# Lists in layer 0 without waits among them, two tail masks on VectorE, and later expert tiles normalised by VectorE and ScalarE

## The chip, the core and the metric

The kernel runs on one core of a Trainium2 chip. The core has five instruction queues that run side by side and meet at semaphores: TensorE (PE, matrix products and transposes into PSUM), VectorE (DVE), ScalarE (ACT), GpSimd (POOL) and SyncE (SP, which here only starts transfers). Each executes its own instructions strictly in order. The metric is the device time of one launch in microseconds, the median of three runs.

## What is computed

The reference is a network of two "metaformer" layers on four images `x` (4, 256, 32, 32) in float32. With 256 channels there are 1024 tokens an image, 4096 in all.

```python
# layer 0
x = x + attention(ln_c(x))     # 8 heads; per row only the dyn_k largest scores stay, then softmax
                               # plus a 3x3 depthwise convolution of v, and a 1x1 projection
t = to_tokens(x)
t = t + moe0(ln_t(t))          # 8 experts 256->256->256 with gelu, each token to its best two
x = from_tokens(t)
# layer 1
x = x + scans(ln_c(x))         # selective scan in four directions, averaged
t = to_tokens(x)
t = t + moe1(ln_t(t))          # 8 experts with a layer norm each, 256->1024->256, best two
```

In the attention, `dyn_k` comes from the data: `dyn_k = floor(1024 * mean(sigmoid(gate(x))))`. `moe0` normalises the tokens before the router and the experts and adds its own input back: `out = tokens + sum of combine * expert(tokens)`.

## The kernel before

The program goes through four stages: attention with routing (0 to about 1975 us), the expert tiles of layer 0 (to about 2222), the scans of layer 1 (to about 3480), and the expert tiles of layer 1 (to the end). The change touches the first two.

**Attention.** The unit is a half: 128 query rows of an image by four heads, 64 halves in all. The order of work is written out by hand as turns `i = 0..71`. In turn `i`, half `i` gets its scores on TensorE, which ScalarE copies to SBUF (`s_n`). VectorE and ScalarE count how many scores lie above a guessed threshold, in this and the following turns (lines 733 and 737, each one pass over 128x1024 scores), and `update` narrows the guess. Half `i - 3` is then finished: VectorE runs `w` and `MAX8` over each of its four score rows (lines 784 and 787), and picks the exact threshold from the window (lines 792 to 798, the result is `last`). GpSimd makes four masks `dr` (line 817), one for each head, 128x1024 in bfloat16: one where the score lies below `last`. Six small operations on GpSimd, `verify` (lines 806 to 811), check the choice. In the next turns two halves of a group form a `Pair`. Its `weights` are computed on TensorE: products of q and k (line 872), onto which the masks are transposed and added as large negative numbers (line 877, with `dr` as the stationary operand). ScalarE takes the exponential (line 885), TensorE the sums (line 895), VectorE divides (lines 904 and 905). The masks of the odd half of a pair have one buffer each, those of the even half two. The last pair, 31, of halves 62 and 63, is made in turn 66.

**Lists.** Once an image is finished, its tokens are routed beside the attention of the following image; images 0, 1 and 2 start at turns 24, 40 and 56. When the places of its tokens are known, `send` (lines 210 to 217) writes the token rows to the slots of their experts, `slots_x0`: for each of 8 blocks of 128 tokens two indirect DMAs (first and second expert), issued by GpSimd. In `behind_masks`, which stands after masks and checks in a turn, images 0 and 1 send one block a turn over 8 turns, and image 2 two blocks a turn in turns 63 to 66. They are called with `group = None`: each such DMA then depends on the one before it, since both write `slots_x0`. The last image is routed after the attention, and its DMAs form a group without dependencies among them ("scatter0").

**Expert tiles of layer 0.** Tokens lie sorted by expert in tiles of 256; there are 36 of them (three more stand ready for very uneven routing and aren't run). Here an automatic scheduler orders the instructions from the program order and its estimates. A tile consists of: `load` (SP starts DMAs for the rows `xs` and the expert's weights, lines 1428 to 1433; `xs` has 6 buffers), `normed` (line 1438, GpSimd, two operations of 128x256 that scale and shift each row into `xn`, which has 2 buffers), `small` (weights of the two experts and biases, VectorE, lines 1449 to 1463), `turned` (four TensorE transposes, line 1445, and a VectorE copy to `xe`, line 1447), `hidden` (TensorE, line 1470, and gelu on ScalarE, line 1472), `result` (TensorE, line 1478; VectorE, line 1481) and `store` (ScalarE, line 1485: an Identity with a scale and a shift for each row; VectorE, line 1487; a GpSimd DMA to `rows_y0`, line 1489).

Other work stands beside the tiles (the loop at line 1948): from tile 14 on, the completion of image 0 and the preparation of its scans; from tile 22 on, that of image 1. To complete an image, `fetched` gathers its tokens' results with 16 indirect DMAs on GpSimd (line 1878), and `completed` transposes them on TensorE (`op`, line 1891) into `x` (VectorE, line 1897). The preparation of the scans (lines 1774 to 1843) uses all engines; it takes exponentials and logarithms on ScalarE between the tiles' gelus, which switches ScalarE's function tables (ACT_TABLE_LOAD).

Of the kernel before, what the change touches and what calls it, by code (L numbers as in the profile page):

```python
# [16 lines left out]
AF = mybir.ActivationFunctionType  # L17
ALU = mybir.AluOpType
# [4 lines left out]
B = 4  # L23
C = 256
# [3 lines left out]
NT = L // P  # L28
# [19 lines left out]
FIRST, SECOND = (2 * (i + 1) * L // T + E - 1 for i in range(2))  # L48
# [14 lines left out]
def metaformer(ctx: ExitStack, tc: tile.TileContext, t: dict, out: bass.AP):  # L63
    nc = tc.nc
# [145 lines left out]
    def send(b, tiles, group):  # L210

        for n in tiles:
            for k in range(2):
                ins = nc.gpsimd.indirect_dma_start(
                    out=slots_x0, out_offset=bass.IndirectOffsetOnAxis(ap=sent[:, k, b * NT + n : b * NT + n + 1],
                                                                       axis=0),
                    in_=xr[b][:, n], in_offset=None).ins
                if group is not None:
                    tc.declare_no_dep(ins, group=group, reason="rows of their own")
                    tc.add_to_no_dep_group(group, ins)  # L220

    def counted(sums, both, tiles):

# [246 lines left out]
    with ExitStack() as st:  # L470
# [23 lines left out]
        for j in range(4):  # L494
            r = slice(32 * j, 32 * j + 32)
# [224 lines left out]
        class Half:  # L720
# [76 lines left out]
                self.last = p2.tile([P, 4], F32, tag="last", name="last")  # L797
                nc.vector.tensor_reduce(self.last, pv, AX.X, ALU.add)

            def verify(self):  # L800


                win = self.win
                sure = p2.tile([P, 4, WIN + 2], F32, tag="sure", name="sure", bufs=1)
                pool = nc.gpsimd.tensor_tensor
                pool(sure[:, :, : WIN + 1], win[:, :, : WIN + 1], win[:, :, 1:], ALU.subtract)
                pool(sure[:, :, WIN + 1], win[:, :, 0], win[:, :, 2], ALU.subtract)
                nc.gpsimd.tensor_scalar(sure, sure, 0.0, None, ALU.is_gt)
                pool(sure[:, :, : WIN + 1], sure[:, :, : WIN + 1], self.hot, ALU.mult)
                pool(sure[:, :, WIN + 1], sure[:, :, WIN + 1], self.group.small[:, self.m], ALU.mult)  # L810
                pool(fine, fine, sure, ALU.add)

            def mask(self, after):
                self.drops = []
                for r in range(4):
                    dr = wk.tile([P, L], BF16, tag=f"dr{self.n}{r}", name="dr", bufs=2 - self.n)
                    ins = nc.gpsimd.tensor_scalar(dr, self.row(r), self.last[:, r : r + 1], None, ALU.is_lt)  # L817
                    if r == 0 and after is not None:

                        tc.add_manual_dep(ins.ins, after.ins.name,  # L820
                                          mybir.DependencyInfo(mybir.DependencyClass.Sync,
                                                               mybir.DependencyReason.DATA))
                    self.drops.append(dr)
# [84 lines left out]
        order = [(b, g, a, n) for b in range(B) for g in range(2) for a in range(NP) for n in range(2)]  # L908
# [13 lines left out]
        for b in range(B):  # L922
            i = b * PER
# [9 lines left out]
        routings = {}  # L933
# [4 lines left out]
        for b in range(B - 1):  # L938
            turn0 = b * PER + 24
# [4 lines left out]
        def behind_masks(i):  # L944
            for turn0, routing in routings.items():
                at = i - turn0
                if at == 1:
                    routing.spread((0, 1))
                if at == 2:
                    routing.spread((2, 3))  # L950
                    routing.root()
                if at == 4:
                    routing.shares()
                    routing.locate()
                if at == 6:
                    routing.fix()
                if routing.b < B - 2 and 7 <= at < 15:
                    send(routing.b, (at - 7,), None)
                if routing.b == B - 2 and 7 <= at < 11:
                    send(routing.b, (2 * at - 14, 2 * at - 13), None)  # L960

        def before_masks(i):
            for turn0, routing in routings.items():
# [53 lines left out]
        def turn(i):  # L1017
            def half(d):
                return halves[i - d] if 0 <= i - d < len(halves) else None

            h0, h1, h2, h3 = (half(d) for d in range(4))

            pair, q = pairs.get((i - 5) // 2 if i % 2 else (i - 6) // 2), 0 if i % 2 else 2
            done = pairs.get((i - 7) // 2) if i % 2 else None

            if h0:
                h0.scores(1)
                h0.take(0)
            before_masks(i)
            beside(i, 0)  # L1030
            if h0:
                h0.count(4, h0.at_guess, (0, 1))
                h0.take(1)
            if pair:
                pair.weights(q)
            if h3:
                h3.window(0)
                h3.window(1)
            if half(1) or half(2):
                to_u(slice(0, 2), FIRST_DVE[1])  # L1040
                update(stay=True)
            if h2:
                h2.keep_threshold()
            if done:
                done.norm()
            if h0:
                h0.count(4, h0.at_guess, (2, 3))
            beside(i, 1)
            if pair:
                pair.exps()  # L1050
                pair.sums(q)
            if h3:
                h3.window(2)
                h3.window(3)
                h3.select()
            if h1:
                h1.count(FIRST_DVE[0], h1.at_state)
            beside(i, 2)
            if pair:
                pair.weights(q + 1)  # L1060
            if h0:
                h0.enter()
            if h1:
                to_u(slice(h1.lane, h1.lane + 1), FIRST_DVE[0])
            after = update(stay=False) if h0 or h1 else None
            if h2:
                h2.count(FIRST_DVE[0], h2.at_last, (0, 1))
            if h3:
                h3.mask(after)
                h3.verify()  # L1070
                if h3.n == 1:
                    pairs[h3.i // 2] = Pair(halves[h3.i - 1 : h3.i + 1], images[h3.b])
            behind_masks(i)
            beside(i, 3)
            if pair:
                pair.exps()
            if h2:
                h2.count(FIRST_DVE[0], h2.at_last, (2, 3))
            if i + 1 < len(order):
                start(i + 1)  # L1080
            if pair:
                pair.sums(q + 1)
            beside(i, 4)
            if h0:
                h0.count(FIRST_DVE[1], h0.at_state)
            if h1:
                h1.count(FIRST_DVE[1], h1.at_state)
# [136 lines left out]
            due(1 << 20)  # L1224

        for h in range(NHALF):
            send(B - 1, range(4 * h, 4 * h + 4), "scatter0")

    def attention_by_bits(st):
        wp = st.enter_context(tc.tile_pool(name="a_w", bufs=1))  # L1230
# [170 lines left out]
    def tiles_of_0(st, name):  # L1401
# [13 lines left out]
        class Tile0:  # L1415
# [19 lines left out]
            def normed(self):  # L1435
                self.xn = pb.tile([P, T // P, C], F32, tag="xn", name="xn")
                for a in range(T // P):
                    nc.gpsimd.tensor_scalar(self.xn[:, a], self.xs[:, a, :C], self.xs[:, a, C + 4 : C + 5],
                                            self.xs[:, a, C + 3 : C + 4], ALU.mult, ALU.add)

            def turned(self):
                tp = ps1.tile([P, CT, T], F32, tag="tp", name="tp")
# [52 lines left out]
    with tc.If(some > 0):  # L1495
# [4 lines left out]
        with tc.If(again > 0):  # L1500
            with ExitStack() as st:
                attention_by_bits(st)
            with tc.tile_pool(name="g_w", bufs=1) as pool_s, tc.tile_pool(name="g_ps", bufs=4, space=PSUM) as pool_p:
                nc.sync.dma_start(slots_x0.rearrange("(a p) c -> p a c", p=P),
                                  blank(pool_s)[:, :W0].unsqueeze(1).to_broadcast([P, (E * BLOCKS + 1) * T // P, W0]))
                space = pool_s.tile([P, L], F32, tag="space", name="space")
                for b in range(B):
                    for h in range(NHALF):
                        wide_bank = pool_p.tile([P, L], F32, tag="w", name="wide_bank", bufs=2)
                        for _ in halved(b, h, space, lambda name: pool_p.tile([P, HALF], F32, tag="m", name=name),  # L1510
                                        lambda: wide_bank):
                            pass
                        send(b, range(4 * h, 4 * h + 4), "scatter0_again")
                for _ in table(space, lambda name: pool_p.tile([P, HALF], F32, tag="m", name=name)):
                    pass
        more_tiles = nc.values_load(extra[0:1, 0:1], min_val=0, max_val=1,
                                    skip_runtime_bounds_check_because="a comparison gives 0 or 1")
        with tc.If(more_tiles > 0):
            with ExitStack() as st:
                Tile0, _, _ = tiles_of_0(st, "mx")  # L1520
# [454 lines left out]
    with ExitStack() as st:  # L1975
# [100 lines left out]
        order = [(b, c, s) for b in range(B) for c in range(CT) for s in range(NS)]  # L2076
# [94 lines left out]
    with ExitStack() as st:  # L2171
# [71 lines left out]
        with ExitStack() as sa:  # L2243
# [16 lines left out]
            b = B - 1  # L2260
# [119 lines left out]
```

## Time and profile before

| | |
|---|---|
| median of three runs | 4077.45 us (4071.04 to 4083.21) |
| profiled run | 4081.9 us, its span 4080.2, clock granted to TensorE 0.879 |
| busy shares | PE 86%, DVE 75%, ACT 69%, POOL 47% |
| list DMAs, line 214, 1850 to 1920 us | 12 DMAs, 12.8 us busy, 17.4 us of waiting for the landing of another |
| masks, line 817, same stretch | 12 masks, 33.9 us busy |
| `xn`, line 1438 | 72 operations, 544 ns at the shortest, 600 in the middle |
| gathers, line 1878, 1975 to 2225 us | 32 DMAs, 40.8 us busy |

Times are microseconds, counted from the start of the profiled span, unless they are marked ns. A profile line of a group gives line, engine, operation, result<-operands with shapes and count, then busy time, mean duration in ns and, after the second bar, how long the engine idled just before these instructions, and what ended most of that. The busy time of DMA instructions on GpSimd is only the time of issuing them. Engines idle for many reasons; what counts for the time of the kernel is where the engine that sets the end of a stage is idle.

### The profile page before, as it was taken

To read this page: it belongs to the slowest core of one execution; us is meant where nothing else is said; L and a number is where in the kernel's file an instruction comes from. 1 tells how busy PE (TensorE), PEld (TensorE's weight loads), DVE (VectorE), ACT (ScalarE), POOL (GpSimd) and SP (SyncE) were. 2 spreads that over 40 slices of the span, in tenths; PEclk is the share of its full clock that TensorE was granted. 3 is DMA by queue.
4 is the path that set the end of the run, shared out by engine and by line. 5 is a ranking of instruction groups with operands and counts; after the bars stand their busy time and mean duration, and the time that the engine had idled before them with its cause. 6 is when DMAs were issued, how large, how long until landed. Compare 5 with 4: busy or idle time off the path is not lost. (4 is left out here: it accounts for less than half of the span.)

```text
span 4080.2 us, 50501 instructions
## 1 busy us (share of the span) xinstructions
PE 3528.6 (86%) x17586; PEld 1968.7 (48%) x17586; DVE 3043.3 (75%) x5411; ACT 2806.1 (69%) x3726; POOL 1925.6 (47%) x1693
## 2 busy tenths in 40 slices
PE   8378888888788888885676999999999999999996
PEld 5144444444354435443554434444444434788885
DVE  2689898989899898985656899899899899411112
ACT  2889999999999998993235566767767667322222
POOL 0155445675548554855454656445445446121111
PEclk8568787788778877887788999999999999999997
DMA  9400093000000000000564434333334324566565
GB/s 276 116 1 1 1 256 90 1 1 26 12 5 1 14 11 9 1 11 22 182 184 127 120 104 133 103 103 126 114 97 128 107 103 141 192 184 188 187 193 189
DMA packets 241819, 393.77 MB, mean 97 GB/s; under 512 B 31888, under 2 KB 182160, under 8 KB 241424
## 3 DMA queue, kind: packets, MB, share of 16 engines
q1 hardware_dynamic: 218016, 340.54, 28.1%
q0 software_dynamic: 19904, 48.48, 3.7%
q8 instruction: 142, 2.33, 0.2%
q10 hardware_dynamic: 3632, 1.40, 0.1%
q14 instruction: 125, 1.02, 0.1%
HBM read 280.41 MB, written 109.94 MB: 96 GB/s over the span
## 5 line engine op out<-in xcount | busy, mean ns | idle before, releaser
L817 POOL TENSOR_SCALAR dr<-s_n,last 128x1024 bf16<-128x1024 f32 x256 | 732.8, 2878 | 701.1 <-DVE state L845 395.2
L733 ACT ACTIVATE junk_a<-s_n,state 128x1024 int8<-128x1024 f32 x448 | 514.7, 1149 | 23.9 <-DVE state L851 7.7
L2052 POOL TENSOR_TENSOR da_c<-prod,come 128x1024 f32<-128x1024 f32 x128 | 248.1, 1938 | 435.3 <-DVE h L2058 384.5
L737 DVE TENSOR_SCALAR_CACHE_REDUCE junk_v<-s_n,state 128x1024 int8<-128x1024 f32 x320 | 408.6, 1277 | 8.8
L2228 ACT ACTIVATE hid<-hp,b 128x256 f32<-128x256 f32 x288 | 133.5, 473 | 355.9 <-PE hp L2226 355.7
L784 DVE SCALAR_TENSOR_TENSOR w<-s_n,win 128x1024 f32<-128x1024 f32 x256 | 354.4, 1384 | 5.3
L787 DVE MAX8 win<-w 128x8 f32<-128x1024 f32 x256 | 314.5, 1228 | 8.8
L885 ACT ACTIVATE ex<-sT 128x1024 f32<-128x1024 f32 x256 | 247.1, 1016 | 106.5 <-PE sT L877 106.5
L2019 POOL TENSOR_TENSOR uu<-dx,bb 128x1024 f32<-128x1024 f32 x127 | 302.7, 2384 | 1.5 <-DMA bb<-bc_d 1.5
L733 ACT ACTIVATE junk_a<-s_n,guess 128x1024 int8<-128x1024 f32 x256 | 294.3, 1149 | 7.2
L2058 DVE TENSOR_TENSOR_SCAN h<-da_c,uu 128x1024 f32<-128x1024 f32 x127 | 288.6, 2272 | 0.0
L2032 DVE TENSOR_TENSOR_SCAN h<-da,uu 128x1024 f32<-128x1024 f32 x127 | 288.3, 2270 | 0.0
L2041 DVE TENSOR_TENSOR_SCAN h<-da,uu 128x1024 f32<-128x1024 f32 x127 | 287.3, 2262 | 0.0
L895 PE MATMUL o_ps<-ex,vT 128*32 128x256 f32 x2048 | 238.3, 449 | 49.0 <-ACT ex L885 41.6
L2003 ACT ACTIVATE da_c<-delta,a_log 128x1024 f32<-128x1024 f32 x128 | 268.4, 2097 | 5.8 <-issue 5.7
L2062 PE MATMUL hp<-h,ident 128*128 128x512 f32 x512 | 248.6, 608 | 22.5 <-DVE h L2058 22.3
L2226 PE MATMUL hp<-xe,w 128*128 128x256 f32 x1152 | 258.6, 381 | 6.9 <-DVE xe L2214 6.7
L2239 POOL DMA_INDIRECT results<-ys,to x72 | 69.8, 970 | 408.9 <-DVE ys L2237 182.2
L2237 DVE TENSOR_TENSOR ys<-yp,b2e 128x512 f32<-128x512 f32 x36 | 24.9, 691 | 315.5 <-PE yp L2234 315.5
L767 ACT COPY s_n<-sp 128x1024 f32<-128x1024 f32 x256 | 245.3, 1003 | 19.0 <-PE sp L759 12.0
L2027 PE MATMUL hp<-da_c,ident 128*128 128x512 f32 x512 | 249.2, 610 | 9.1 <-POOL da_c L2052 6.5
L2234 PE MATMUL yp<-w2e,hid 128*128 128x256 f32 x1152 | 255.9, 379 | 0.0
(643 smaller groups left out, 7798.7 us busy)
## 6 DMA issues: line engine op xcount, KB each, us to landing
cb<-bc_d SPq DMA_DIRECT2D x128, 512.0 KB, 4.1
bb<-bc_d SPq DMA_DIRECT2D x127, 512.0 KB, 5.0
w<-in_w SPq DMA_DIRECT2D x36, 1024.0 KB, 5.2
w2e<-in_w SPq DMA_DIRECT2D x36, 1024.0 KB, 5.7
slots_x<-zeros SPq DMA_DIRECT2D x1, 33669.0 KB, 138.9
slots_x<-zeros SPq DMA_DIRECT2D x1, 33282.0 KB
w<-in_w SPq DMA_DIRECT2D x72, 256.0 KB, 3.1
xs<-slots_x SPq DMA_DIRECT2D x36, 261.0 KB, 3.3
```

What stands on the lines that cost most here:

```text
L733: nc.scalar.activation(junk, self.row(r), AF.Sign, bias=thr, scale=-1.0, accum_out=u)
L737: nc.vector.tensor_scalar(junk, self.row(r), thr, None, ALU.is_lt, ALU.add, accum_out=u)
L784: nc.vector.scalar_tensor_tensor(w, self.row(r), self.win[:, r, 0:1], self.row(r), ALU.is_gt if r < LAST_DVE else ALU.is_ge, ALU.subtract, ...
L787: nc.vector.max(out=self.win[:, r, 1:], in_=w)
L817: ins = nc.gpsimd.tensor_scalar(dr, self.row(r), self.last[:, r : r + 1], None, ALU.is_lt)
L2003: nc.scalar.activation(grid(self.da_c), cols_flipped(self.prep.delta[:, self.c]), AF.Exp, scale=self.decay)
L2019: nc.gpsimd.tensor_tensor(self.uu[:, 0], self.prep.dx[:, self.c], self.bb, ALU.mult)
L2032: nc.vector.tensor_tensor_scan(rows.rearrange("p r w -> p (r w)"), self.da, self.uu[:, 0], 0.0, ALU.mult, ALU.add)
L2041: nc.vector.tensor_tensor_scan(hs[:, ::-1], self.da[:, ::-1], self.uu[:, 0][:, ::-1], 0.0, ALU.mult, ALU.add)
L2058: nc.vector.tensor_tensor_scan(hs, self.da_c, self.uu[:, 1], 0.0, ALU.mult, ALU.add)
L2226: nc.tensor.matmul(hp[:, f % 2], self.w1[:, c, ts(f, P)], self.xe[:, c], start=(c == 0), stop=(c == CT - 1))
L2234: nc.tensor.matmul(yp[:, a], self.hid[:, f, ts(a, P)], self.w2[:, f, :], start=(f == 0), stop=(f == NF - 1))
```

## The change

The change has three parts.

1. `send` becomes a generator that hands back control after each DMA, and every DMA belongs to the group "scatter0", with no dependencies among them. A new function `lists(i)` yields the DMAs of two blocks in each of the four turns from the seventh after an image's first turn on, for images 0, 1 and 2 alike. `verify` takes this generator and issues one DMA between its own operations. So the lists of images 0 and 1 take four turns of four DMAs instead of eight of two; those of image 2 keep their turns.
2. For the last three halves (61, 62, 63), the masks of rows 2 and 3 are made by VectorE instead of GpSimd, right behind rows 0 and 1 in program order. These are 6 of 256 masks.
3. In the expert tiles of layer 0, from tile 14 on, the first half of `xn` is made by VectorE (the same multiply and add) and the second by ScalarE (Identity with scale and bias); GpSimd makes them up to tile 13.

```diff
-                if group is not None:
-                    tc.declare_no_dep(ins, group=group, reason="rows of their own")
-                    tc.add_to_no_dep_group(group, ins)
+                tc.declare_no_dep(ins, group=group, reason="rows of their own")
+                tc.add_to_no_dep_group(group, ins)
+                yield
...
-            def verify(self):
+            def verify(self, between):
...
                 pool(sure[:, :, : WIN + 1], win[:, :, : WIN + 1], win[:, :, 1:], ALU.subtract)
+                next(between, None)
                 pool(sure[:, :, WIN + 1], win[:, :, 0], win[:, :, 2], ALU.subtract)
+                next(between, None)
                 nc.gpsimd.tensor_scalar(sure, sure, 0.0, None, ALU.is_gt)
+                next(between, None)
                 pool(sure[:, :, : WIN + 1], sure[:, :, : WIN + 1], self.hot, ALU.mult)
+                next(between, None)
                 pool(sure[:, :, WIN + 1], sure[:, :, WIN + 1], self.group.small[:, self.m], ALU.mult)
+                assert next(between, True)
                 pool(fine, fine, sure, ALU.add)

             def mask(self, after):
...
-                    ins = nc.gpsimd.tensor_scalar(dr, self.row(r), self.last[:, r : r + 1], None, ALU.is_lt)
+                    eng = nc.vector if self.i >= len(order) - 3 and r >= 2 else nc.gpsimd
+                    ins = eng.tensor_scalar(dr, self.row(r), self.last[:, r : r + 1], None, ALU.is_lt)
...
-                if routing.b < B - 2 and 7 <= at < 15:
-                    send(routing.b, (at - 7,), None)
-                if routing.b == B - 2 and 7 <= at < 11:
-                    send(routing.b, (2 * at - 14, 2 * at - 13), None)
+
+        def lists(i):
+            for turn0, routing in routings.items():
+                at = i - turn0 - 7
+                if 0 <= at < NT // 2:
+                    yield from send(routing.b, (2 * at, 2 * at + 1), "scatter0")
...
-                h3.verify()
+                h3.verify(lists(i))
...
             def normed(self):
                 self.xn = pb.tile([P, T // P, C], F32, tag="xn", name="xn")
                 for a in range(T // P):
-                    nc.gpsimd.tensor_scalar(self.xn[:, a], self.xs[:, a, :C], self.xs[:, a, C + 4 : C + 5],
-                                            self.xs[:, a, C + 3 : C + 4], ALU.mult, ALU.add)
+                    scale, shift = self.xs[:, a, C + 4 : C + 5], self.xs[:, a, C + 3 : C + 4]
+                    if a and self.i >= FIRST - 1:
+                        nc.scalar.activation(self.xn[:, a], self.xs[:, a, :C], AF.Identity, bias=shift, scale=scale)
+                    else:
+                        (nc.vector if self.i >= FIRST - 1 else nc.gpsimd).tensor_scalar(
+                            self.xn[:, a], self.xs[:, a, :C], scale, shift, ALU.mult, ALU.add)
```

`send` for the last image, and for a routing that is repeated in a rare case, is called in a loop that runs the generator to its end; the former is otherwise as before.

More of the change, by code (lines that the diff above doesn't have):

```diff
@@ L1226, in metaformer @@
         for h in range(NHALF):
-            send(B - 1, range(4 * h, 4 * h + 4), "scatter0")
+            for _ in send(B - 1, range(4 * h, 4 * h + 4), "scatter0"):
+                pass
     def attention_by_bits(st):
@@ L1512, in metaformer @@
                             pass
-                        send(b, range(4 * h, 4 * h + 4), "scatter0_again")
+                        for _ in send(b, range(4 * h, 4 * h + 4), "scatter0_again"):
+                            pass
                 for _ in table(space, lambda name: pool_p.tile([P, HALF], F32, tag="m", name=name)):
```

## The prediction

> **What bounds the kernel now.** I read the page first. Its busy shares (PE 86%, POOL 47%) are averages over unlike stages, and its chain of waits lies almost wholly in the last stage, so neither tells what GpSimd costs. The groups do: the masks of line 817 are the costliest.
>
> ```profile
> span 4080.2 us, 50501 instructions
> L817 POOL TENSOR_SCALAR dr<-s_n,last 128x1024 bf16<-128x1024 f32 x256 | 732.8, 2878 | 701.1 <-DVE state L845 395.2
> ```
>
> One mask takes 2.88 us, but GpSimd idled 701 us before masks, mostly for VectorE: over the attention as a whole it has slack, and shortening its work there is worth nothing. So I looked for places where TensorE waits for it, and found two.
>
> The first is the end of the attention, after the last score has been taken. Three timelines, GpSimd, VectorE, TensorE (start, duration, engine, line; in brackets the idle time before and its releaser):
>
> ```profile
> 1868.50 0.96 POOL L214 DMA_INDIRECT slots_x<-x,sent  x1 [1.84 <-DMA slots_x<-x,sent]
> 1871.43 1.96 POOL L214 DMA_INDIRECT slots_x<-x,sent  x1 [1.97 <-DMA slots_x<-x,sent]
> 1873.43 11.31 POOL L817 TENSOR_SCALAR dr<-s_n,last 128x1024 bf16<-128x1024 f32 x4
> ...
> 1896.36 11.30 POOL L817 TENSOR_SCALAR dr<-s_n,last 128x1024 bf16<-128x1024 f32 x4
> ```
>
> ```profile
> 1869.98 0.18 DVE L798 TENSOR_REDUCE last<-pv 128x4 f32<-128x32 f32 x1
> ...
> 1883.62 0.19 DVE L798 TENSOR_REDUCE last<-pv 128x4 f32<-128x32 f32 x1
> ```
>
> ```profile
> 1899.28 0.61 PE L877 MATMUL sT<-drop,dr 128*128 128x128 bf16 x4 [13.30 <-POOL dr L817]
> 1902.09 0.61 PE L877 MATMUL sT<-drop,dr 128*128 128x128 bf16 x4 [2.20 <-POOL dr L817]
> 1904.91 0.61 PE L877 MATMUL sT<-drop,dr 128*128 128x128 bf16 x4 [2.21 <-POOL dr L817]
> 1907.72 0.50 PE L877 MATMUL sT<-drop,dr 128*128 128x128 bf16 x3 [2.21 <-POOL dr L817]
> ```
>
> VectorE has the threshold of half 62 at 1870.16 and that of half 63 at 1883.81; GpSimd begins the masks at 1873.43 and 1896.36. It is late because a turn costs it 11.3 us of masks, 1.6 us of checks and about 10.5 us of list DMAs, each of which waits some 1.9 us until the one before has landed. TensorE stands 19.9 us for it.
>
> The second is the expert tiles of layer 0 (1975 to 2222 us). The waits of that stretch (engine, line, releaser: total, times, longest), then busy time by windows:
>
> ```profile
> PEld tp L1445 <- POOL xn L1438: 39.5, 6, 18.2
> PE tp L1445 <- POOL xn L1438: 36.3, 3, 17.8
> POOL xn L1438 <- PE tp L1445: 34.5, 18, 5.5
> ```
>
> ```profile
> 2060.00:2090.00 30.00, 10.66 (x49) 7.88 (x47) 8.63 (x31) 5.24 (x11) 24.95 (x24) 0.71 0.73 185
> 2090.00:2120.00 30.00, 28.67 (x139) 23.33 (x140) 20.51 (x67) 10.40 (x20) 9.20 (x14) 0.90 0.53 151
> 2121.00:2150.00 29.00, 23.96 (x87) 14.63 (x87) 13.68 (x37) 14.03 (x22) 24.27 (x24) 0.91 0.71 175
> 2150.00:2175.00 25.00, 17.20 (x71) 12.66 (x69) 16.71 (x41) 20.03 (x26) 8.99 (x11) 0.91 0.38 109
> ```
>
> The columns are length, then TensorE, its weight loads, VectorE, ScalarE, GpSimd, clock, DMA share, GB/s. In the first window GpSimd is full with the 16 gathers of image 0 (line 1878), the next `xn` stands behind them, and TensorE works 10.66 of 30 us. Of its wait, one stretch of 17.84 ends at 2088.44. In the third the gathers of image 1 do the same, with a wait of 5.04 that ends at 2147.63. In the fourth ScalarE is full (20.03 of 25), with seven table loads of 1.28 us.
>
> **What the Trainium skill says.** "VectorE: DVE Perf Modes", section on the perf-mode tier table: `tensor_scalar` on fp32 in SBUF goes at twice the rate (1227 ns for 2048 elements). The trace has no such mask; VectorE copies of 128x2 (180 ns) and 128x256 (299) give 0.47 ns an element, which agrees. "SBUF — State Buffer", Who interferes with whom: such an op, and one with two SBUF inputs, contends with GpSimd for a shared port, and the second to issue blocks wholly. The trace shows less: the two-input line 784 takes 1.46 to 1.78 us beside masks and 1.28 alone, while masks of 2.83 run on undisturbed. "Perfetto Trace Analysis", DMA Instruction — SWDGE: the end shown for a GpSimd DMA is that of writing its descriptors. This agrees: line 214 shows 0.96 to 1.96 us and lands 1.9 later. "ScalarE: Activation LUTs", Table sets: identity is in every set, so a normalising Identity needs no table load; line 1485, of this kind, runs among the gelus here without one.
>
> **Part 1, lists, and part 2, masks, belong together at the tail.** Lists of images 0 and 1 sit in turns where GpSimd idled 6 to 14 us before its masks; four DMAs of about 1.27 (0.96 to 1.96, plus gaps) are 5 us instead of two waiting ones. I cost these at nothing; the cover is VectorE's counting, and without it they cost 5 us in each of 8 turns.
>
> For image 2 the order leaves each DMA only a wait on one eight DMAs earlier, long landed. GpSimd's turn becomes 5.66 (two masks) + 1.6 + 4 x 1.27 = 12.3 us instead of 23. Turn 64 still begins at 1849.76 (released by a count), and GpSimd is free at 1862, before the threshold of half 62.
>
> The two masks on VectorE stand right behind the threshold, ahead of counts. From below one costs 0.66 (0.18 + 1024 x 0.47 ns), from above 1.28 (line 737, one pass over the same operand) plus 0.5 of contention. I take 0.7 + 0.25 = 0.95. VectorE has no gap from 1849.5 to 1883.8, so the four before the threshold of half 63 delay it by 3.8. Its own excess beside masks (line 784: 0.18 + 0.24 + 0.50 + 0.24 + 0.24, two small ops 0.41 + 0.43, sum 2.24) halves with the masks, -1.1. Threshold at 1883.81 + 3.8 - 1.1 = 1886.5. GpSimd, free by 1884.5, makes masks 0 and 1 until 1892.3; VectorE's two are ready by then. TensorE's other products of that step take 0.8, ScalarE's two exponentials 2 x 1.02, partly beside: they end at about 1894.6, before it was 1909.34. **Gain 14.7**, bounds 11.4 (masks at 1.78) and 15.9 (0.66). What is late next is VectorE's selection, not GpSimd. From 1907.7 TensorE runs nearly without a gap to 1940, so the gain is carried forward.
>
> **Part 3, normalising.** For tiles 14 to 35, 44 operations of 0.54 to 0.60 leave GpSimd; each tile gets one on VectorE (0.3, the 128x256 copy) and one on ScalarE (0.54, line 1485). A steady tile takes 4.35 us, of which TensorE works 4.16; VectorE idles 0.9, ScalarE is busy 2.0. There both are hidden.
>
> At the first gathers the 17.84 goes, but the transposes `op` of image 0 stand in TensorE's queue behind tiles 20 and 21. TensorE now comes to the last of them at about 2085, the gathers land at about 2089, and it waits some 4 there. These transposes ran at 2105.88: gain 17. At the second gathers most of the 5.04 goes, +4. Against it stands ScalarE's full stretch. In the new order ScalarE's halves of tiles 28, 29 and 30 stand behind the outputs of tile 27 and ahead of a table load and tile 28's gelu. Tile 28's transposes wait for the first of these; TensorE had done them earlier. From there: 0.54 (Identity) + 0.5 (transposes, hop) + 0.9 (copy, hop) + 1.3 (first products, hop) = 3.2 until that gelu, where a table load of 1.28 stood: 2 late, and about 2 of TensorE's work no longer done in advance: -4. Later tiles run in pairs, in which TensorE waits for `xe`, 0.2 each: -0.6. **Gain 16.4**, bounds 8 (gathers landing later with loads competing, another 4 lost behind table loads) and 21 (nothing lost).
>
> Scans and layer 1 are unchanged. Sum 14.7 + 16.4 = 31.1. The profiled run took 4081.9 (1.7 around its span): 4050.8. The median of three is 4.45 lower: 4077.45 - 31.1 = **4046**.
>
> **Rivals.**
> - *The stall at the tiles only changes its name* (gathers, then table loads): `op` sits in TensorE's in-order queue, and 20 of 25 us on ScalarE lie right behind. Against: 17.84 is far more than the 4 that I find. Gain 14.7 + 3: 4060. Chance 0.16.
> - *The tail gives little*: VectorE's masks block on GpSimd's, 2.83 each for four, 11 of the 14.7 gone, as the skill's page would have it. Line 784's 0.5 speaks against. Gain 4 + 16: 4057. Chance 0.10.
> - *It doesn't act*: descriptors written while VectorE holds the port take as long as the waits they replace, 3 us each, so that lists and gathers still set the pace. One of 1.96 is a hint, eleven of 1 speak against. Gain 5: 4072. Chance 0.07.
> - *Slower*: ScalarE executes in order, and its half of `xn` waits with a gelu queued behind it, for a load or for TensorE to free the buffer. GpSimd spent 34.5 us in 18 waits for the latter, 1.9 each, and 23.7 for loads, harmlessly. Over 22 tiles the gain is eaten at 1.4 us each, and the kernel is slower by over 0.3% from 2.0; at 2.5 it is 55 - 31 = 24 slower: 4101. Against: the order puts these halves behind a tile's outputs, when the buffer is mostly free, and six `xs` buffers let loads run ahead. Chance 0.05.
>
> **How the numbers follow.** The forecast has 0.62; its own range is 4036 (both upper bounds, 37, and 4 of scatter) to 4058 (both lower bounds, 19.4). Runs of before lie from 4071 to 4083, so a median can be off by 4. The range 4034 to 4064 takes in the first two rivals. What this kernel's measurement can tell is about 0.3%, 12 us: faster 0.86 (0.62 + 0.15 + 0.09), same 0.09, slower 0.05.
>
> **What would show it.** Right: line 877 waits 1 to 3 us for a mask after the last threshold, none of 13; list DMAs follow one another without a landing between; TensorE's transposes no longer wait for GpSimd after tile 13, but `op` waits a few us for a gather; VectorE's mask row near 0.95. Wrong: a mask over 2 us on VectorE, ScalarE waiting for loads or TensorE ahead of line 1438's successor, over 10 us before `op`, or a stage after 2230 us that changes its length.

## The result and the profile after

The changed kernel takes **4048.24 us** (median of four runs, 4039.79 to 4051.12), the kernel before beside it 4076.81 (four runs as well): the ratio is 0.9926, with an interval of 0.9905 to 0.9947. The forecast was 4046.

In the profiled run the span went from 4080.2 to 4045.4 us, 34.8 less. I cut both traces at the same four instructions: GpSimd's first mask of half 61 (the tail begins), ScalarE's third pair of exponentials of pair 31 (its masks are behind it), the first transpose of tile 0, and the scan of line 2041 (2055 after), which starts when the last tile's output has landed.

| stretch | before | after | difference |
|---|---|---|---|
| start to the tail's first mask | 1849.76 | 1849.24 | -0.5 |
| tail of the attention | 72.21 | 58.35 | -13.9 |
| last image's projection and routing | 57.6 | 57.6 | 0 |
| expert tiles of layer 0 | 248.2 | 232.2 | -16.0 |
| scans and layer 1 | 1852.5 | 1848.0 | -4.5 |

The first and the last row are scatter: in all the profiles of this study the first lies between 1837.6 and 1853.2 us, the last between 1847.7 and 1853.3, in no order that follows the edits. So a total of one run says little here, and the stretches in between carry what follows. They are read from one profile of each kernel: where kernels have the same code for a stretch, the tail differs by about 1 us between them and the tile stage by 3 to 6.

The tail after, in the timelines of GpSimd, VectorE and TensorE (start, duration, engine, line; idle before and releaser in brackets):

```profile
1870.25 7.20 POOL L823 TENSOR_SCALAR dr<-s_n,last 128x1024 bf16<-128x1024 f32 x2 [7.36 <-DVE last L798]
1877.42 0.23 POOL L806 TENSOR_TENSOR sure<-win 128x32 f32<-128x32 f32 x1
1877.82 1.05 POOL L214 DMA_INDIRECT slots_x<-x,sent  x1 [0.16 <-issue]
1878.90 1.15 POOL L808 TENSOR_TENSOR sure<-win 128x4 f32<-128x4 f32 x1
1880.20 1.00 POOL L214 DMA_INDIRECT slots_x<-x,sent  x1 [0.15 <-issue]
...
1885.75 0.65 POOL L816 TENSOR_TENSOR fine<-fine,sure 128x36 f32<-128x36 f32 x1
1886.38 5.67 POOL L823 TENSOR_SCALAR dr<-s_n,last 128x1024 bf16<-128x1024 f32 x2
```

```profile
1870.12 2.28 DVE L823 TENSOR_SCALAR dr<-s_n,last 128x1024 bf16<-128x1024 f32 x2
...
1878.71 1.28 DVE L784 SCALAR_TENSOR_TENSOR w<-s_n,win 128x1024 f32<-128x1024 f32 x1
...
1884.57 0.19 DVE L798 TENSOR_REDUCE last<-pv 128x4 f32<-128x32 f32 x1
1884.86 1.42 DVE L823 TENSOR_SCALAR dr<-s_n,last 128x1024 bf16<-128x1024 f32 x2
```

```profile
1889.28 0.61 PE L883 MATMUL sT<-drop,dr 128*128 128x128 bf16 x4 [3.46 <-POOL dr L823]
1892.10 1.35 PE L883 MATMUL sT<-drop,dr 128*128 128x128 bf16 x11 [2.21 <-POOL dr L823]
```

The list DMAs follow one another at 0.15 us and an operation of the checks, where 1.9 us of landing stood. Masks of half 62 start with their threshold. TensorE's wait of 13.30 has become 3.46. But the masks of half 63 start with no idle before them, 1.6 us behind a threshold that is ready at 1884.76: GpSimd is still the last. Part of the reason stands in these lines: its check at 1878.90 takes 1.15 us, where the same operation takes 0.21 in the next turn, and ends at 1880.05, just behind VectorE's line 784, which ends at 1879.99.

The tile stage after. First the waits of TensorE from 1965.2 to 2197.42 us (total, times, longest), then a window of 30 us over the first gathers, as in the kernel before (length, PE, PEld, DVE, ACT, POOL busy with counts, clock, DMA share, GB/s), then three lines of TensorE's timeline:

```profile
PE hp L1483 <- DVE xe L1460: 13.9, 10, 3.0
PE tp L1458 <- POOL xn L1451: 13.4, 1, 13.4
...
PE tp L1458 <- ACT xn L1449: 3.1, 1, 3.1
PE op L1905 <- DMA y<-rows_y,slot: 1.4, 2, 1.2
```

```profile
2048.00:2078.00 30.00, 25.43 (x126) 20.48 (x127) 22.77 (x73) 13.94 (x29) 24.16 (x22) 1.00 0.96 264
```

```profile
2048.31 1.56 PE L1491 MATMUL yp<-w,hid 128*128 128x256 f32 x6 [0.35 <-ACT hid L1485]
2051.96 1.56 PE L1483 MATMUL hp<-xe,w 128*128 128x256 f32 x6 [0.79 <-DVE xe L1460]
2057.95 1.56 PE L1491 MATMUL yp<-w,hid 128*128 128x256 f32 x6 [0.35 <-ACT hid L1485]
```

GpSimd is as full with gathers as before (24.16 of 30), but TensorE now works 25.43 us beside them instead of 10.66. Of its waits for GpSimd's `xn` only the one for tile 0 is left, 13.4, which ends where the stage begins and is older than the change. In its place come waits for `xe` (8.0 before, 13.9 now), for the gathers at `op` (1.4) and one for ScalarE's half of tile 28. The third fence shows the tiles running in pairs: `yp` to `yp` is 9.64 us for two tiles, where one took 4.345 before.

### The profile page after: what moved, and what is told of

The parts are those of the page before. It is cut to its first block, busy times and chain, and to the rows that moved or that the text cites. A ratio compares the mean times of both kernels' runs of the same rounds, so it can differ in the third digit from the quotient of the medians.

```text
span 4045.4 us, 50460 instructions
## 1 busy us (share of the span) xinstructions
PE 3522.2 (87%) x17586; PEld 1963.0 (49%) x17586; DVE 3049.1 (75%) x5439; ACT 2818.0 (70%) x3748; POOL 1894.3 (47%) x1643
## 5 line engine op out<-in xcount | busy, mean ns | idle before, releaser
L823 POOL TENSOR_SCALAR dr<-s_n,last 128x1024 bf16<-128x1024 f32 x250 | 719.7, 2895 | 734.8 <-DVE state L851 377.2
L2034 ACT COPY uu<-uu 128x1024 f32<-128x1024 f32 x127 | 252.3, 1987 | 2.5 <-POOL uu L2033 2.5
```

What stands on the lines that cost most here:

```text
L823: ins = eng.tensor_scalar(dr, self.row(r), self.last[:, r : r + 1], None, ALU.is_lt)
```

## Experiments

Every kernel below computes everything. The intervals of the totals reach 4 us (e2) to 13 us (e6) to either side; so the stretches are given beside them.

**Each part alone.** e1 is the changed kernel with part 1 only:

```diff
-                    eng = nc.vector if self.i >= len(order) - 3 and r >= 2 else nc.gpsimd
+                    eng = nc.vector if False else nc.gpsimd
...
-                    if a and self.i >= FIRST - 1:
+                    if False:
...
-                        (nc.vector if self.i >= FIRST - 1 else nc.gpsimd).tensor_scalar(
+                        nc.gpsimd.tensor_scalar(
```

> Part 1 alone (lists between the checks, all masks and xn on GpSimd as before). My theory: in the tail a turn costs GpSimd 11.3 us of masks + 7.1 of checks and lists = 18.4 us, against 14.6 between VectorE's thresholds. So masks of half 62 begin with their threshold (1870.2), those of half 63 wait for GpSimd until about 1889 and end at about 1900.5. The exponentials behind the last mask end near 1902.2 (before 1909.3, after 1894.6): 7 us gained, nothing in the expert tiles; about 4070. Rival A (the waits between lists are the whole of the tail's loss): the exponentials end near 1895, 4062. Rival B (the masks are the bound, lists stand in their shade): under 2 us gained, 4076.

e2 has part 2 only; its `normed` is that of e1, its lists those of before:

```diff
-                tc.declare_no_dep(ins, group=group, reason="rows of their own")
-                tc.add_to_no_dep_group(group, ins)
+                if group is not None:
+                    tc.declare_no_dep(ins, group=group, reason="rows of their own")
+                    tc.add_to_no_dep_group(group, ins)
...
-                h3.verify(lists(i))
+                h3.verify(iter(()))
...
+                if routing.b < B - 2 and 7 <= at < 15:
+                    for _ in send(routing.b, (at - 7,), None):
+                        pass
+                if routing.b == B - 2 and 7 <= at < 11:
+                    for _ in send(routing.b, (2 * at - 14, 2 * at - 13), None):
+                        pass
```

> Part 2 alone (six masks on VectorE, lists waiting one for another as before, xn on GpSimd). My theory: a turn costs GpSimd 5.7 to 7.2 us of masks + 12.1 of checks and waiting lists, and GpSimd stays the last: masks of half 63 begin near 1889.5 and the exponentials end near 1898 (before 1909.3, after 1894.6): 11.5 us gained, 4065. Together with part 1 alone (7) that is more than the 14.7 of both, since both relieve the same queue and VectorE is next. Rival A (waits between lists are the whole loss): about 4 us gained, 4072. Rival C (the parts add up): part 1 and part 2 sum to 14.7.

e3 has parts 1 and 2 (the `normed` of e1), e4 part 3 only (the mask line of e1, the lists of e2).

> Parts 1 and 2 without part 3 (xn on GpSimd in all tiles). My theory: exponentials behind the last mask end at 1894.6 as after, the expert tiles of layer 0 take as long as before (first transposes to the last scan start behind them: 248 us), total 14.7 less than before: 4062. TensorE again waits about 18 us for xn at the first gathers and 5 at the second. Rival (part of the tail's gain is lost or won later): the total differs from 4062 by over 5.

> Part 3 alone (lists and masks as before). My theory: the tail as before (exponentials end at 1909.3), the tile stage 16 us shorter (248 to 232 us between the first transposes and the scan that starts behind the last store), 4061. Rival (part 3 pays only together with the earlier lists): under 10 us. Also: if the scans and layer 1, which no part touches, take 3 to 4 us less than before here too, that is scatter from run to run or a real consequence of part 3; if they do so in only one of e1 to e4, it is scatter.

| | median | ratio to before, interval | tail | tile stage |
|---|---|---|---|---|
| before | 4077.63 | | 72.2 | 248.2 |
| e1, lists | 4071.9 | 0.9981 (0.997 to 0.9993) | 64.8 | 250.1 |
| e2, masks | 4067.44 | 0.9977 (0.9969 to 0.9986) | 62.1 | 247.2 |
| e3, lists and masks | 4057.91 | 0.9952 (0.9935 to 0.9969) | 58.9 | 250.3 |
| e4, normalising | 4059.02 | 0.9953 (0.9937 to 0.9968) | 71.5 | 236.2 |

The last rounds of masks in GpSimd's timeline, of e1 and then of e2, show why:

```profile
1869.11 11.31 POOL L823 TENSOR_SCALAR dr<-s_n,last 128x1024 bf16<-128x1024 f32 x4 [1.87 <-DVE last L798]
1886.88 11.31 POOL L823 TENSOR_SCALAR dr<-s_n,last 128x1024 bf16<-128x1024 f32 x4
```

```profile
1865.41 7.20 POOL L824 TENSOR_SCALAR dr<-s_n,last 128x1024 bf16<-128x1024 f32 x2 [2.98 <-DVE last L799]
1884.99 5.67 POOL L824 TENSOR_SCALAR dr<-s_n,last 128x1024 bf16<-128x1024 f32 x2
```

In both, the masks of half 62 wait for VectorE and those of half 63 don't: GpSimd is behind, in e1 by 5.0 us (the threshold is ready at 1881.87), in e2 by 5.2 (1879.84). So both parts relieve the same queue. Alone they give 7.4 and 10.1 us of tail, together 13.3, less than the 17.5 of a sum: rivals A, B and C fall. Part 3 gives 12.0 us in the tile stage without the others (248.2 to 236.2) and 18.1 beside them (250.3 in e3, 232.2 in the changed kernel), which its scatter doesn't tell apart. That the tile stage of e1 to e3 stays within 3 us of that before shows that nothing of the tail is paid back there.

**The early lists.** e8 takes those of images 0 and 1 back to their eight turns with waits (`send` as in e2), and leaves image 2's as changed:

```diff
+                if routing.b < B - 2 and 7 <= at < 15:
+                    for _ in send(routing.b, (at - 7,), None):
+                        pass
...
-                if 0 <= at < NT // 2:
+                if routing.b == B - 2 and 0 <= at < NT // 2:
                     yield from send(routing.b, (2 * at, 2 * at + 1), "scatter0")
```

> The changed kernel, but with the lists of images 0 and 1 as in the kernel before (one block a turn over eight turns behind the checks, each DMA waiting for the one before); image 2's as changed. My theory: these stand where GpSimd waits for VectorE, and cost nothing either way: total that of after within its scatter (4048 +- 4), waits of masks for VectorE shorter by what the lists take. Rival (the waiting lists delay masks in mid-attention): 5 us in some of the eight turns each, up to 16 turns: 4060 or more.

It took 4046.11 us (4036.95 to 4053.34), its tail 58.8, its tile stage 235.1, and the tail began at 1850.59 us. This is the changed kernel's time. The part of the change that acts on images 0 and 1 is worth nothing that can be measured. The cover shows too: with lists that wait for one another again, GpSimd idles 708.7 us ahead of its masks in e8, against 734.8 in the changed kernel.

**ScalarE's half.** e5 leaves both halves of `xn` to VectorE:

```diff
-                    if a and self.i >= FIRST - 1:
+                    if False:
```

> The changed kernel, but both halves of xn on VectorE from tile 14 on, none on ScalarE. My theory: ScalarE's half is what makes TensorE work in pairs of tiles (9.6 us a pair instead of 8.7) and what tile 28's transposes wait 3.1 us for behind the table loads. Without it tiles 14 to 20 take 4.35 us each and op is reached some 4 us earlier, where the wait for the gathers grows by about as much (from 1.4 to 4 or 5); the 3.1 goes, and the pairs after tile 30 too (about 2). Tile stage (first transposes to the scan behind the last store) 232 to 226 us, total about 5 to 6 less than after. Rival (VectorE needs ScalarE's help: its added 0.3 us a tile is late for xe, or its pass over the shared port slows the gathers' descriptors): tile stage 232 or more, TensorE waits for xe or xn from VectorE, and op later than after.

It took 4042.08 us (ratio 0.9905, 0.9885 to 0.9926), its tile stage 224.8. TensorE's timeline and then its waits, 1961.7 to 2186.47 us:

```profile
2039.29 1.13 PE L1483 MATMUL hp<-xe,w 128*128 128x256 f32 x4 [0.19 <-ACT hid L1485]
2043.63 1.13 PE L1483 MATMUL hp<-xe,w 128*128 128x256 f32 x4 [0.19 <-issue]
...
2069.04 0.33 PE L1905 MATMUL op<-ident,y 128*128 128x128 f32 x1 [1.78 <-DMA y<-rows_y,slot]
2071.23 0.85 PE L1905 MATMUL op<-ident,y 128*128 128x128 f32 x5 [1.86 <-DMA y<-rows_y,slot]
```

```profile
PE hp L1483 <- DVE xe L1460: 8.4, 4, 2.8
PE op L1905 <- DMA y<-rows_y,slot: 3.6, 2, 1.9
```

The pairs are gone (4.34 from tile to tile), the wait at `op` has grown from 1.4 to 3.6 as expected, and so the end of `op`, counted from tile 0, moved by only 2.3 us (112.7 to 110.4). The other 5 us come behind it, where the wait for ScalarE's half of tile 28 (3.1) and the pairs are gone. The three kernels with this code (e5, e7, e10) have tile stages of 224.8, 229.3 and 223.6 us, the four with ScalarE's half 232.2 to 236.3. VectorE, with 44 more operations of 0.42 us than before, is late nowhere that shows. The rival falls.

**The last four masks.** e6 gives all four masks of half 63 to VectorE:

```diff
-                    eng = nc.vector if self.i >= len(order) - 3 and r >= 2 else nc.gpsimd
+                    eng = nc.vector if self.i >= len(order) - 3 and r >= (0 if self.i == len(order) - 1 else 2) else nc.gpsimd
```

> The changed kernel, but all four masks of the last half (63) on VectorE, at 0.7 us each. My theory: in the changed kernel GpSimd, not VectorE, was the last in the tail (free 1.6 us behind the threshold, then two masks of 2.83). With four on VectorE the masks are done 2.8 us behind the threshold instead of 7.3; but the division of the pair before stands behind them on VectorE and the sums need its result, about 5 us behind the threshold. From the first tail mask to the end of the exponentials behind the last: 45.4 to about 41 us; total 4 less than after. Rival (TensorE isn't bound by the masks any more): within 1 of 45.4.

VectorE's timeline of e6, then TensorE's:

```profile
1884.15 0.19 DVE L798 TENSOR_REDUCE last<-pv 128x4 f32<-128x32 f32 x1
1884.45 2.75 DVE L823 TENSOR_SCALAR dr<-s_n,last 128x1024 bf16<-128x1024 f32 x4
```

```profile
1886.92 1.07 PE L883 MATMUL sT<-drop,dr 128*128 128x128 bf16 x16
1889.46 0.80 PE L901 MATMUL o_ps<-ex,vT 128*32 128x256 f32 x8 [1.47 <-DVE att L911]
```

Four masks take 2.75 us, TensorE has no wait for a mask left, and the sums wait 1.47 for the division that stands behind the masks. The tail is 52.9 us, 5.5 less than in the changed kernel (from the first mask to the end of the exponentials just behind the masks 41.65, where I expected about 41). The total, 4047.49 (4026.78 to 4052.93), scatters too much to show 5 us, so that the 4 us expected of it are not shown.

**Both together, and one step further.** e7 has the edits of e5 and e6, and e10 is the same kernel again. e9 adds:

```diff
             yield from fetched(b, y, range(NHALF))
-            yield from pause(24)
+            yield from pause(24 if b else 32)
```

> The two edits before together. They sit in different stages, so they should add: 4 + 5.5 less than after, about 4038. Rival (what one stage gains the next gives back, as at the gathers): no less than the better of the two alone.

> The kernel of e7 (four last masks and all later xn on VectorE) with the pause between the gathers of image 0 and its transposes op 32 steps long instead of 24, some one and a half tiles. My theory: TensorE waits 4.5 us for the gathers at op only because op stands too early in its queue; two tiles put ahead of it hide that, and the tile stage becomes 4 us shorter than in e7 (229 and, of the same kind, 225 in e5): 4027. Rival (the preparation of the scans behind op, with ScalarE's table loads, is what bounds the stage, so moving it back costs what the wait gives): tile stage 226 to 232, 4031 or more.

> The kernel of e7 once more, beside e9 on the same chip: 4031 within 4. If it lies above 4038, e7's lead over e5 (4042) was scatter and the edits don't add.

| | median | ratio to before, interval | tail | tile stage |
|---|---|---|---|---|
| e7 | 4031.02 | 0.9884 (0.9862 to 0.9906) | 52.9 | 229.3 |
| e10 | 4037.82 | 0.9893 (0.9876 to 0.9911) | 51.9 | 223.6 |
| e9 | **4018.99** | 0.9856 (0.9841 to 0.9872) | 52.9 | 211.0 |

In the stretches both edits keep their effect side by side: the tail is that of e6, the tile stage that of e5. The totals don't settle whether they add: e7's 4031 lies 11 us below e5's 4042, but the repeat, e10, missed the expected 4031 by 7 us, and 4037.82 is just below the 4038 above which I had meant to call the lead scatter. e9 is the fastest of all: 19 us below e10, which ran beside it, and 12 below e7, where I had expected 4. The windows over the tile stage of before, after, e10 and e9, in this order (the columns as above):

```profile
1979.50:2227.72 248.22, 195.22 (x836) 148.48 (x836) 155.03 (x483) 101.17 (x178) 119.25 (x140) 0.88 0.61 172
```

```profile
1965.20:2197.42 232.22, 190.35 (x836) 144.62 (x836) 159.76 (x505) 112.31 (x201) 90.84 (x96) 0.93 0.63 184
```

```profile
1959.50:2183.07 223.57, 190.31 (x836) 144.66 (x836) 165.75 (x528) 101.20 (x178) 88.95 (x96) 0.93 0.66 190
```

```profile
1951.10:2162.10 211.00, 180.62 (x836) 139.46 (x836) 165.16 (x530) 98.52 (x176) 88.47 (x96) 0.95 0.69 202
```

Of the 12.6 us between e10 and e9, the wait at `op` gives 3.4 (4.7 there, 1.3 in e9), which is the theory. TensorE's other waits mostly shift: those for `xe` fall from 8.8 to 3.3, those of the products `hp` for ScalarE's gelu grow from 10.0 to 17.7. `op` doesn't even end earlier: 114.8 us after tile 0 in e9, 112.4 in e10. What is won lies behind it, and most of it, 9.7 us, is TensorE's own busy time: the same 836 matmuls take 180.6 instead of 190.3. The clock accounts for nearly all of that. Cut at the changes of the granted clock, which is either full or half in these traces, 27.3 us of TensorE's work fall into time at half clock in e10 and 9.8 in e9. If a matmul takes twice as long there, the difference is worth 8.7 us (an estimate, which the next section tests). In e9 ScalarE also loads its tables twice less in this stage (10 loads instead of 12). Why the later place of `op` leaves so little work at half clock, no run here shows.

## Why the prediction was right, point by point

**Part 1 and 2, the tail: 14.7 predicted, 13.9 measured** (13.3 to 13.9 in four profiles with both parts). The mechanism was right, and so was the time at which GpSimd begins the last masks: 1886.5 predicted, 1886.38 measured. But the two terms behind it were both off.
- VectorE: I took 0.95 us for a mask; the six mean 0.89. Five took 0.75 and one 1.61. That one began while GpSimd was at a mask; of another that began so, GpSimd bore the cost, with a mask of 3.76 instead of 2.83. I halved its excess beside masks; line 784 has none left (1.28 to 1.31 us, where 1.46 to 1.78 stood). So the threshold came at 1884.76, not at 1886.5 (0.5 of this is the earlier start of the tail).
- GpSimd: "free by 1884.5" was 1.9 too early. A turn was to cost it 12.3 us. The last one, with VectorE almost idle, took 12.15 (1886.38 to 1898.53), but that of half 62 took 16.1. All that is longer there began while VectorE was at a mask or at line 784, which reads two operands: two masks took 7.20 instead of 5.67, three operations of the checks 0.65 to 1.15 instead of 0.2 to 0.3, and a list DMA 1.74 instead of 1.03, together 4.0 us. The small ones ended 0.06 to 0.11 us behind VectorE's operation. The prediction counted this contention on VectorE's side alone and put it at nothing on GpSimd's. Without these 4.0 us GpSimd would have been free at about 1882.4 (an estimate), ahead of the threshold.
- So "what is late next is VectorE's selection, not GpSimd" was wrong. GpSimd was late by 1.6 us, and its two masks cost 5.7 where VectorE's cost 1.4. TensorE's waits for them were 3.46 and 2.21 us, where 1 to 3 had been named. e6 shows what this was worth: 5.5 us.

That the sum came out nevertheless is luck: the threshold came earlier and GpSimd later than forecast, by about as much.

The early lists at nothing: right (e8). That the two parts belong together: right, and e1 and e2 show how much they overlap.

**Part 3, the tiles: 16.4 predicted, 16.0 measured**, 14.0 as the mean over four profiles with it (232.2, 236.2, 236.3, 235.1) against four without (248.2, 250.1, 247.2, 250.3).
- "At the first gathers the 17.84 goes" and op waits for the gathers: right. Counted from tile 0, the end of `op` moved from 127.8 to 112.7, by 15.1 where I had 17. The gathers landed 2 to 3 us later than I had put them, and so `op` ended later; TensorE waited 1.4 there, not 4, because it came late itself.
- It came late by the step that I mis-sized: "later tiles run in pairs, in which TensorE waits for `xe`, 0.2 each". They run so from tile 13 on, and it is 0.47 each (9.64 for two tiles against 8.69). The prediction called both new operations hidden in a steady tile and gave pairs to later tiles only; some nine tiles of 0.47 ahead of `op` used up nearly all of the cover that the gathers gave. VectorE's half took 0.43 us instead of 0.3, ScalarE's 0.59 instead of 0.54. e5 shows that it is ScalarE's half that brings the pairs about.
- Behind `op` I had +4 for the second gathers, -4 at the table loads, -0.6: nothing on balance. Measured: 120.4 us before, 119.5 after; as means of four profiles, 121.1 without part 3 and 122.0 with it. The wait for ScalarE's half of tile 28 is there (3.1), the wait for VectorE's copy behind it too (2.0).

**The sum: 31.1 predicted; 28.6 between the medians of the runs, 29.8 in the two stretches of the profile.** The rivals: the stall at the tiles didn't just change its name, and ScalarE's order cost 3.1 us once, not 1.4 a tile. Descriptors are written in 1.0 to 1.05 us; one of the twelve list DMAs of the tail took 1.74, begun beside line 784 as the one of 1.96 before. Of the four masks of VectorE ahead of the last threshold, three weren't held up, and one by 0.86 us, not by 2.83. The Trainium skill, "SBUF — State Buffer", Who interferes with whom, has it that the later of two such operations waits for the whole of the earlier one. In this trace that fits GpSimd's small operations, which ended just behind VectorE's, and not VectorE's mask, which took 1.61 us beside a mask of 3.33.

**What the prediction didn't see** is what a stall does to the clock of TensorE. It priced 17.84 us of waiting at 17.84. Of the 16.0 us in the tile stage, 11.1 are idle time of TensorE (53.0 before, 41.9 after), and 4.9 are its busy time for the same 836 matmuls, at a mean clock of 0.93 instead of 0.88. The forecast of 16.4 was made of waits; that it met the sum is luck in this part too. The Trainium skill has this under "TensorE: Matmul & The Clock Gate", Part 1: the array's clock is gated back after idle time, and released again by sustained work. The windows agree: 0.71 in the 30 us with the stall before, 1.00 in the 30 us over the same gathers after. Closer, a window and a line of TensorE's timeline of the kernel before:

```profile
2072.60:2093.10 20.50, 3.87 (x11) 2.85 (x12) 2.92 (x10) 0.48 (x1) 16.38 (x18) 0.50 0.52 118
```

```profile
2089.91 2.08 PE L1470 MATMUL hp<-xe,w 128*128 128x256 f32 x4 [0.78 <-DVE xe L1447]
```

The stall began at 2070.60; the clock stood at half from 2072.6 to 2093.1, 4.7 us past the stall's end, and four products of `hp` took 2.08 us there, where they take 1.13 at full clock. This stall left only 3.87 us of work at half clock; most of such work lay elsewhere in the stage. In all it was 38.6 us before and 25.2 after. If a matmul takes twice as long at half clock, that is worth 6.7 us (an estimate; 4.9 are measured). The estimate holds across profiles: TensorE's busy time less half of its work at half clock is 175.9 us before, 177.7 after, 176.7 in e10 and 175.7 in e9.

## What to carry to other kernels

Look at a queue's work for each stage between two outputs of its producer, not over the whole kernel: GpSimd idled 700 us ahead of these masks and was still the bound in the last turns, and two cures for one queue don't add (7.4 and 10.1 us alone, 13.3 together). When work leaves a queue, ask who is last now and by how much: here moving two more masks paid another 5.5 us, and giving ScalarE no half at all shortened the tile stage by 7. When two engines run side by side, price the contention for both: here the one that looked free, GpSimd, lost 4.0 us in one turn. And an in-order queue turns the place of an instruction into a cost: putting the consumers of a slow gather some one and a half tiles later made the stage 12.6 us shorter, though it hid a wait of only 3.4.

## What the runs showed that I had not expected

- VectorE makes a 128x1024 mask in 0.75 us (four in a row in 2.75), GpSimd in 2.83, a factor of 4. Side by side both lose, but not alike. Of two VectorE masks begun during one of GpSimd's, one took 1.61 us and one 0.75, so that neither waited for the whole of GpSimd's. GpSimd's small operations begun during a mask or line 784 of VectorE ended just behind it. Beside VectorE's MAX8 (line 787) and division (line 910) GpSimd's operations took their usual time (0.23 and 0.21 us for checks, 1.05 for a list DMA).
- Sharing the normalising of a tile between two engines changed the order that the scheduler gave a third: with ScalarE's half TensorE works in pairs of tiles (9.64 us), without it one by one (2 x 4.345), though neither VectorE nor ScalarE is full.
- The same 836 matmuls of the tile stage took between 180.6 us (e9) and 197.8 (e3), the less the less of them ran at half clock (9.8 and 43.2 us).
